# A transformer block's prelude in single words and another order, two small products on GpSimd, and the last MLP batch in halves

## The chip, the cores and the metric

The kernel runs on one core of a Trainium2 chip. Its time is the device time of one execution in microseconds (us). Five engines take part: TensorE (PE; its weight loads are listed as PEld), VectorE (DVE), ScalarE (ACT), GpSimd (POOL) and SyncE (SP), which only issues DMAs. Each engine works through its own instructions in order and waits on semaphores for the others.

## The reference

The kernel computes one block of a diffusion transformer on 16 batches of 256 tokens of width 256, all in float32: self attention with 16 heads, cross attention to a context, and an MLP of width 1024.

```python
c_proj = silu(c) @ W_mod + b_mod
shift_a, scale_a, gate_a, shift_m, scale_m, gate_m = split(c_proj, 6)
x_norm = ln(x) * (1 + scale_a) + shift_a
q, k, v = split(x_norm @ W_qkv + b_qkv, 3)            # 16 heads of 16
attn = softmax(q @ k.T * scale) @ v
x = x + gate_a * (attn @ W_proj + b_proj)
q_c = ln(x) @ W_qc + b_qc;  k_c, v_c = split(ln(context) @ W_kvc + b_kvc, 2)
x = x + (softmax(q_c @ k_c.T * scale) @ v_c) @ W_cproj + b_cproj
x_norm2 = ln(x) * (1 + scale_m) + shift_m
x = x + gate_m * (gelu(x_norm2 @ W_mlp1 + b_mlp1) @ W_mlp2 + b_mlp2)
```

## The kernel before, in words

**Units and beats.** The work is cut into 32 attention units (self attention of batch 0 to 4 first, units 0 to 4, then self and cross attention in turn). Each unit has eight beats, (n, 0) to (n, 7). In the beats of unit n the scores of unit n + 1 are multiplied (`s_tile`, row maxima by DVE into `mx`), the transposed scores of unit n (`t_part`) go to the exponential on ACT, and projections and transposes of later units fill PE. After every fourth beat the products with the values follow (tile `o`). Beats (-1, 0) to (-1, 7) hold unit 0's scores alone: at even beats both score tiles lie in the two banks of `st` and one DVE maximum of 1024 columns takes them, at odd beats they lie in `sp` with two maxima of 512.

**Precision by halves.** Each float32 operand is split into a high and a low part of a faster type, and three products are added (`mm3`). For the scores, K and Q of a unit are stacked in one tile, `big[n % 3]`: rows for high, high again and low parts, a row of ones, and a row that takes the negated row maxima. A stack is filled by DMA from the tiles `h_...` and `l_...`: six copies of 128 KB for K and six for Q. In the words of the prelude, `x` and `y` are the two copies of the high part, `l` that of the low part, and 0 or 1 the half of the heads; a `p` at the end means that GpSimd issues the copy instead of the sync queue. Unit 2 and later units send theirs in their beats.

**The prelude** is written out by hand in the string `PRE`, whose words call functions one after another, and in the table `SL`, whose words run after the beat that is their key. All engines keep the order of these words. The words that matter:

- `b12`, `b4`, `b9`, ...: so many 128x128 products of a zero tile (`busy`, two instructions each);
- `load`, `ld2`, `ld3`, `ld4`: the first weight and x loads; `z0kp`, `z1qp`, ...: GpSimd clears half of a `big` tile; `one0`: the rows of ones;
- `L0a`, `L0b`, `L0c`/`L0d`: a layernorm's statistics (DVE), mean and power (DVE, then GpSimd: `rs_s`), and its application (`c` on GpSimd, `d` on DVE: `xn_s`);
- `T0t`, `T0h`, `T0l`/`T0p`: transpose (PE), scaled high part (ACT), low part (DVE, or ACT and GpSimd);
- `scale`, `shift`, `bq`, `bk`, `bv`, `mods`: sixteen-column products for modulation and biases (`cols`: PE, then one DVE add); `sc1` and `sc2` add one on DVE;
- `hik`, `lok`, ...: split of a weight (ACT, then GpSimd; `lov` on DVE);
- `K0a`, `K0m`, `K0h`, `K0l`: first and second half of the K projection (PE, six matmuls each), high part (ACT), low part (DVE); `K1b` is `m` and `h` in one; likewise Q; `V0a`, `V0b`: values;
- `M0`: transpose of the row maxima, ACT, and their send by the sync queue; `wm`, `gm`: the MLP gate's loads, and its product.

`rest` takes the next step of a generator, `setup_rest`: loads of W_mod's gate columns, W_proj, W_cproj and biases; the attention gate `ga`; the bias product `pb` with a multiply by the gate and a store to `gd`; `cb`; loads of the cross attention's weights; and five weight splits on GpSimd. The multiplies of gate and bias (16x256, tile `gb` in `setup_rest`, tile `gB` in `f_gm`) run on DVE.

**The MLP** works in chunks (b, c), four to a batch. `mlp_second` adds chunk after chunk into `m.po`, two PSUM banks, one for each half of the tokens: those of `sp` (two tiles) for even batches and of `st` (one tile) for odd ones. After the last chunk DVE multiplies each half by the gate (`mt`), adds the residual (`y`), and one DMA of 256 KB stores the batch.

Where the trace shows L51, that is the line of the helper which issues every ordered instruction; tiles tell the instructions apart.

Of the kernel before, what the change touches and what calls it, by code (L numbers as in the profile page):

```python
# [21 lines left out]
def pixart_block(  # L22
# [8 lines left out]
    B, N, H = x.shape  # L31
# [3 lines left out]
    NT = N // P  # L35
    KC = H // P
# [58 lines left out]
    BMOD, BQKV, BQC, BKVC, BM1 = 0, 12, 18, 20, 24  # L95
# [5 lines left out]
    def tok(ap, b):  # L101
        return ap[b].rearrange("(t p) h -> p t h", p=P)
# [33 lines left out]
    st = psum.tile([P, 2, 512], F32, tag="st", name="st", bufs=1)  # L136
    sp = [psum.tile([P, 512], F32, tag=f"s{r}", name=f"s{r}", bufs=1) for r in range(2)]
# [73 lines left out]
    def setup_rest():  # L211
        gb = work.tile([B, 2, 2, H], F32, tag="pt", name="gb", bufs=5)
        gA, bb = gb[:, 0], gb[:, 1]
        bc = const.tile([1, H], F32, name="bc")
        wg, wp = stage(W_mod, 2 * H, "wga", "g", 3), stage(W_proj, 0, "wp_f", "g", 3)
        SP.dma_start(bb[:, 0], b_mod[2 * H:3 * H].partition_broadcast(B))
        SP.dma_start(bb[:, 1], b_proj.partition_broadcast(B))
        SP.dma_start(bc, b_cproj.partition_broadcast(1))
        wcp = stage(W_cproj, 0, "wcp_f", "x1", 7)
        yield  # L220
        pst = ps_gen("ps_ga")
        for k in range(KC):
            PE.matmul(pst[:B, :H], sT[:, k], wg[:, k], start=(k == 0), stop=(k == KC - 1))
        DVE.tensor_tensor(gA[:, 0], pst[:B, :H], bb[:, 0], ALU.add)
        yield
        pst = ps_gen("ps_pb")
        for k in range(KC):
            PE.matmul(pst[:B, :H], bqkv[:, 4 + k], wp[:, k], start=(k == 0), stop=(k == KC - 1))
# [3 lines left out]
        yield  # L232
        pst = ps_gen("ps_cb")
        for k in range(KC):
            PE.matmul(pst[:1, :H], bT[:, BKVC + 2 + k:BKVC + 3 + k], wcp[:, k],
                      start=(k == 0), stop=(k == KC - 1))
        DVE.tensor_tensor(bc, pst[:1, :H], bc, ALU.add)
        SP.dma_start(cd, bc)
        yield
        wkc, wqc = stage(W_kvc, 0, "wkc_f", "g", 3), stage(W_qc, 0, "wqc_f", "c", 2)  # L240
        wvc = stage(W_kvc, H, "wvc_f", "x1", 7)
        yield
        split(Wp[0], Wp[1], wp)
        yield
        split(Wkc[0], Wkc[1], wkc)
        yield
        split(Wqc[0], Wqc[1], wqc)
        yield
        split(Wvc[0], Wvc[1], wvc)
        yield  # L250
        split(Wcp[0], Wcp[1], wcp)

    wm = []

# [427 lines left out]
    def side(home, r):  # L685
        return home[r] if isinstance(home, (list, tuple)) else home[:, r]
# [164 lines left out]
    NCH = NF // 2  # L851
# [98 lines left out]
    for u in units:  # L950
        build_pre(u)
        build_post(u)
    at = defaultdict(list)
    rest = setup_rest()

    u0, u1 = units[:2]
    def one_rows(i):
# [3 lines left out]
    u2 = units[2]  # L961
    word = {}
# [45 lines left out]
    word["rest"] = lambda: next(rest, None)  # L1008
    word["vone"] = lambda: [POOL.memset(v[:, :, :, HD:], 1.0) for v in vts]
    for n, f in (("load", f_load), ("silu", f_silu), ("turn", f_turn), ("brow", f_brow),  # L1010
                 ("scale", f_scale), ("sc1", f_sc1), ("shift", f_shift),
                 ("wm", f_wm), ("mods", f_mods), ("sc2", f_sc2), ("gm", f_gm)):
        word[n] = f
    for i in range(3):
# [8 lines left out]
    for i in range(3):  # L1023
        b = i if i < 2 else 0
# [159 lines left out]
    last, o, q = units[-1], units[-1].post, units[-2].post  # L1184
# [86 lines left out]
```

## Time and profile before

| | us |
|---|---|
| median of three runs | 743.31 |
| the three runs | 748.72, 743.31, 743.25 |
| the profiled execution, its time | 744.65 |
| its span in the profile | 742.9 |

The span runs from the first to the last instruction in the profile; the execution's time holds what lies around it too. The mean granted clock of TensorE over the span is 0.999. The page has 25,296 instructions, and PE's 10,144 matmuls carry the time. The rows that are shown below have one of these forms: in the chain of waits "start, length, what"; in the timeline "start, length, engine, line, operation, tiles, count", and in square brackets the idle time before it and what ended it; in the groups "count | busy us, mean ns | idle before"; in the table of stretches the window, its length, and for each engine its busy time with the number of instructions, then the granted clock, the DMA engines' share and GB/s.

### The profile page before, as it was taken

The numbers are of one execution on the slowest core, as the hardware profiler recorded it, in microseconds if no ns is written. First come the engines' busy times: TensorE is split into PE (matmuls) and PEld (weight loads), VectorE is DVE, ScalarE is ACT, GpSimd is POOL, SyncE is SP. The second block draws the span as 40 slices with busy tenths as digits, with TensorE's granted clock in tenths as the row PEclk, the third lists the DMA queues.
The fourth block names the chain that finished last, engine by engine and source line by source line (L and its number), as shares of the span: only waits on it lengthen the run. The fifth ranks groups of instructions, "written<-read, shape, count | busy, mean of one in ns | idle before, by whom it ended". The sixth has DMA issues, their size and how long they took to land.

```text
span 742.9 us, 25296 instructions
## 1 busy us (share of the span) xinstructions
PE 733.8 (99%) x10144; PEld 648.6 (87%) x10144; DVE 575.4 (77%) x1188; ACT 564.0 (76%) x979; POOL 538.3 (72%) x569
## 2 busy tenths in 40 slices
PE   9999999999999999999999999999999999999997
PEld 8778888888888888888888888888889999999997
DVE  4888888888889898888989888888726566666662
ACT  3268898888888888888888888898886666666663
POOL 6757678869687686968769798798647766666652
PEclk9999999999999999999999999999999999999999
DMA  6754454543545454354545545455113122131310
GB/s 203 203 147 136 127 144 131 143 117 103 154 114 153 131 144 140 94 165 113 149 133 143 158 125 159 122 155 151 59 60 101 58 69 76 55 86 44 86 57 30
DMA packets 89049, 87.98 MB, mean 118 GB/s; under 512 B 8610, under 2 KB 84676, under 8 KB 88932
## 3 DMA queue, kind: packets, MB, share of 16 engines
q1 hardware_dynamic: 88468, 85.58, 40.8%
q8 instruction: 80, 1.31, 0.8%
q0 software_dynamic: 192, 0.52, 0.3%
q10 hardware_dynamic: 272, 0.26, 0.1%
q14 instruction: 37, 0.30, 0.1%
HBM read 26.97 MB, written 8.46 MB: 48 GB/s over the span
## 4 chain that ended last, share of the span: by engine, by line
PE 93%; DVE 2%; POOL 2%; DMA 1%; issue 1%; ACT 1%; SPq 0%; POOLq 0%; DVEq 0%; ACTq 0%
PE s L51 18%; PE st L51 16%; PE o L51 16%; PE ph L51 11%; PE ps_qc L51 4%; PE ps_q L51 4%; PE ps_kc L51 3%; PE ps_v_c L51 3%; PE ps_P_s L51 3%; PE ps_k L51 3%; PE ps_v_s L51 2%; PE ps_P_c L51 2%; PE psT_q L51 1%; PE psA_s L51 1%; PE psT_m L51 1%; PE ps_h L51 1%
## 5 line engine op out<-in xcount | busy, mean ns | idle before, releaser
L51 DVE TENSOR_REDUCE mx<-s 128x2 f32<-128x512 f32 x504 | 324.7, 684 | 64.5 <-PE s L51 58.1
L51 ACT ACTIVATE pt<-st 128x1024 f32<-128x1024 f32 x252 | 258.9, 1027 | 17.3 <-PE st L51 11.6
L51 PE MATMUL s<-big 63*128 63x256 f32 (+1 forms) x1024 | 184.8, 298 | 0.7 <-DVE mx L51 0.6
L51 PEld LDWEIGHTS s<-big 63*128 63x128 f32 (+1 forms) x1024 | 133.4, 186 | 20.0 <-DVE l_kc L51 6.6
L51 PE MATMUL st<-big 64*128 64x256 f32 (+1 forms) x1024 | 134.3, 298 | 0.3 <-ACT pt L51 0.2
L51 POOL TENSOR_TENSOR hl<-hf,hh 128x512 fp32r<-128x512 f32 x64 | 84.6, 1325 | 64.8 <-ACT hh L51 64.7
L51 PE MATMUL o<-pt,v 128*32 128x256 f32 x2048 | 123.8, 382 | 0.0
L51 PEld LDWEIGHTS st<-big 64*128 64x128 f32 (+1 forms) x1024 | 96.2, 185 | 15.8 <-issue 12.9
L51 PEld LDWEIGHTS o<-pt,v 128*32 128x32 f32 x2048 | 60.0, 109 | 41.5
L51 ACT ACTIVATE hf<-ph,bT 128x256 f32<-128x256 f32 x114 | 47.8, 473 | 27.6 <-PE ph L51 27.6
L51 ACT ACTIVATE hh<-ph,bT 128x256 fp32r<-128x256 f32 x114 | 47.8, 471 | 22.5 <-PE st L51 11.8
L51 ACT COPY oT<-o 128x512 f32<-128x512 f32 x63 | 36.9, 586 | 33.3 <-PE o L51 33.3
L51 DVE TENSOR_SCALAR xn_m<-x,mv_m,rs_m 128x256 f32<-128x256 f32 x28 | 24.0, 901 | 32.4 <-POOL rs_m L51 32.4
L51 PE MATMUL s<-big,hh 128*128 128x256 f32 x256 | 46.7, 281 | 0.0
L51 PE MATMUL st<-big,hh 128*128 128x256 f32 x256 | 46.6, 281 | 0.0
L51 PE MATMUL ph<-wkch,wself 128*128 128x256 f32 x224 | 44.9, 284 | 0.0
L51 PE MATMUL ph<-wqch,wself 128*128 128x256 f32 x224 | 44.7, 284 | 0.0
L51 PE MATMUL ps_k<-xTh_s,wself 64*128 64x256 f32 (+1 forms) x232 | 43.9, 295 | 0.0
L51 PE MATMUL ps_q<-xTh_s,wself 64*128 64x256 f32 (+1 forms) x240 | 39.7, 283 | 0.4 <-DVE l_q L51 0.4
L51 POOL TENSOR_SCALAR xn_c<-c,mv_c,rs_c 128x256 f32<-128x256 f32 x32 | 39.0, 1227 | 1.7
L51 PE MATMUL ps_P_s<-wself,xTh_as 64*128 64x256 f32 x256 | 39.1, 282 | 0.0
L51 PEld LDWEIGHTS st<-big,hh 128*128 128x128 f32 x256 | 39.0, 188 | 0.0
(244 smaller groups left out, 2516.9 us busy)
## 6 DMA issues: line engine op xcount, KB each, us to landing
big<-h_kc SPq DMA_DIRECT2D x64, 128.0 KB
big<-h_qc SPq DMA_DIRECT2D x64, 128.0 KB
big<-h_k SPq DMA_DIRECT2D x62, 128.0 KB
big<-h_q SPq DMA_DIRECT2D x62, 128.0 KB
big<-l_k SPq DMA_DIRECT2D x32, 128.0 KB
big<-l_q SPq DMA_DIRECT2D x32, 128.0 KB
g<-gd SPq DMA_DIRECT2D x16, 256.0 KB
c<-in_ctx_dram SPq DMA_DIRECT2D x16, 256.0 KB
```

The costliest lines, as they stand in the source:

```text
L51: i = f(*a, **k)
```

## The change

The generator `setup_rest` becomes single functions, each with a word of its own: `lg`, `lp`, `lc`, `lx` (loads), `ga`, `pb`, `gs`, `cb`, and `sp0` to `sp4` (splits). `PRE` and `SL` get another order. In it:

- unit 0's stack is cleared after `load`; the loads of `rest` and x2 are spread over the prelude;
- T0t stands before `scale`; the zero products are b12, b4, b5, b3, b9 in place of b12, b4, b4, b9;
- L1d stands behind `bk`; L2a and L2b stand in the prelude before unit 1's low parts;
- GpSimd clears unit 1's stack (`z1qp`, `z1kp`) around its copy of K0; its two copies of Q0 (`Q0y0p`, `Q0y1p`) come behind both and behind L2's power;
- of unit 1's twelve copies two are issued before the beats, the others in beats (-1, 0) to (-1, 4), the last of them (`Q1l1`) behind M0's send; all of them go by the sync queue;
- `bv` and V0a stand before Q1; K2a moves from beat (-1, 5) to (-1, 6), `sc2` to (0, 2), `z2qp` to (-1, 7); the splits run in beats (0, 0), (0, 2), (0, 3), (0, 6) and (1, 4).

The two multiplies of gate and bias go from DVE to GpSimd. In `mlp_second` the banks of even and odd batches are swapped, and for the last batch each half of the tokens is multiplied, added and stored by itself, between the matmuls of the two halves.

```diff
-'PRE': 'z0qp z0kp load rest ld2 one0 silu b12 brow L0a turn L0b b4 L0d scale T0t sc1 hik lok L1a T0h L1b T0l b4 shift hiq K0a L1d bk loq K0m K0h K0x0 K0x1 K0y0p K0y1p T1t K0l T1h K0l0 K0l1 bq T1l Q0a Q0m Q0h Q0x0 Q0y0p Q0x1 Q0y1p Q0l Q0l0 Q0l1 z1kp z1qp K1a K1b hiv lov Q1a Q1b K1x0 K1x1 K1y0 K1y1 K1l K1l0 K1l1 Q1x0 Q1x1 Q1y0 Q1y1 Q1l Q1l0 Q1l1 L2a L2b L2c V0a V0b bv b9 ld3'
-'SL': {(-1, 0): 'V1a', (-1, 1): 'T2t T2h T2p vone z2kp z2qp', (-1, 2): 'V1b', (-1, 3): 'rest wm', (-1, 4): 'M0 rest one1 ld4', (-1, 5): 'K2a L3a', (-1, 6): 'K2m L3b L3p L3c', (-1, 7): 'mods sc2 one2 rest', (0, 0): 'gm rest', (0, 1): 'rest', (0, 4): 'rest', (0, 6): 'rest', (1, 0): 'rest', (1, 5): 'rest'}
+'PRE': 'load z0kp silu b12 turn brow L0a z0qp L0b b4 L0d T0t hik scale lok sc1 lg L1a b5 T0h L1b T0l ld2 one0 shift b3 K0a bk hiq lc L1d lp L2a K0m loq K0h T1t K0y0p T1h K0l K0x0 bq hiv K0l0 T1l z1qp K0x1 K0l1 Q0a Q0m K1a K0y1p lov Q0h Q0l Q0x1 K1b Q0l0 bv z1kp V0a Q0l1 Q0x0 Q1a Q1b L2b Q1y0 K1x0 V0b K1l b9 Q0y0p Q0y1p Q1l'
+'SL': {(-1, 0): 'L2c ld3 K1l0 K1y1', (-1, 1): 'Q1l0 T2t Q1y1 V1a T2h Q1x0 K1l1 K1x1 T2p', (-1, 2): 'wm V1b Q1x1 z2kp vone', (-1, 3): 'ga K1y0', (-1, 4): 'pb M0 Q1l1 ld4 gs L3a', (-1, 5): 'L3b L3p one1', (-1, 6): 'one2 K2a L3c K2m', (-1, 7): 'z2qp mods cb', (0, 0): 'gm lx sp0', (0, 2): 'sp1 sc2', (0, 3): 'sp3', (0, 6): 'sp2', (1, 4): 'sp4'}
...
-        DVE.tensor_tensor(gA[:, 1], pst[:B, :H], bb[:, 1], ALU.add)
-        DVE.tensor_tensor(gA[:, 1], gA[:, 1], gA[:, 0], ALU.mult)
-        SP.dma_start(gd[:, 0:2], gA)
+        DVE.tensor_tensor(gA[0][:, 1], pst[:B, :H], gA[1][:, 1], ALU.add)
+
+    def f_gs():
+        POOL.tensor_tensor(gA[0][:, 1], gA[0][:, 1], gA[0][:, 0], ALU.mult)
+        SP.dma_start(gd[:, 0:2], gA[0])
...
-        DVE.tensor_tensor(gB[:, 1], gB[:, 1], gB[:, 0], ALU.mult)
+        POOL.tensor_tensor(gB[:, 1], gB[:, 1], gB[:, 0], ALU.mult)
         SP.dma_start(gd[:, 2:4], gB)
...
-            m.po = [side((sp, st)[b % 2], t)[:, :H] for t in range(NT)]
+            m.po = [side((st, sp)[b % 2], t)[:, :H] for t in range(NT)]
+        done = c == NCH - 1
+        if done:
+            t1 = work.tile([P, NT, H], F32, tag="t1", name=f"mt_{b}")
+            y = work.tile([P, NT, H], F32, tag="x1", name=f"y_{b}", bufs=7)
         for t in range(NT):
             mm3_tok(m.po[t], hT, t, [W2[0][:, 2 * c:2 * c + 2], W2[1][:, 2 * c:2 * c + 2]],
-                    kn=2, start=(c == 0), stop=(c == NCH - 1))
-        if c == NCH - 1:
-            t1 = work.tile([P, NT, H], F32, tag="t1", name=f"mt_{b}")
+                    kn=2, start=(c == 0), stop=done)
+            if done and b == B - 1:
+                DVE.tensor_tensor(t1[:, t], m.po[t], m.g[:, 0], ALU.mult)
+                DVE.tensor_tensor(y[:, t], m.xg[:, t], t1[:, t], ALU.add)
+                SP.dma_start(tok(out, b)[:, t], y[:, t])
+        if done and b < B - 1:
             for t in range(NT):
                 DVE.tensor_tensor(t1[:, t], m.po[t], m.g[:, 0], ALU.mult)
-            y = work.tile([P, NT, H], F32, tag="x1", name=f"y_{b}", bufs=7)
             DVE.tensor_tensor(y, m.xg, t1, ALU.add)
             SP.dma_start(tok(out, b), y)
```

More of the change, by code (lines that the diff above doesn't have):

```diff
@@ new lines, in pixart_block @@
+    E_ = {'CUT': 8, 'LN': {'s': 'pool', 'c': 'pool', 'q': 'pool'}, 'ON': (1, 1, 1), 'L0': -16, 'L1': 1, 'S0': -7, 'A0': 0, 'T0': 1, 'S1': 5, 'A1': 7, 'L2': 9, 'T1': 9, 'S2': 32, 'AP': 23, 'DV': (0, 1), 'HP': (1, 0), 'BZ': {}, 'AV': {1: [(1, 2), (1, 3)], 9: [(0, 0), (0, 1)]}, 'AHEAD': (0, 0, 0, 0, 0, 2), 'TW': {(21, 6): 'cb', (23, 5): 'u0', (23, 7): 'u1', (25, 2): 'u2', (27, 3): 'u3', (27, 7): 'h2a', (28, 0): 'l2 h0p u5', (28, 2): 'h1p', (28, 4): 'h3p', (28, 7): 'u4 u6', (29, 0): 'l3d', (29, 1): 'l0', (29, 2): 'l1', (29, 7): 'h5p', (30, 1): 'u7 h6d h7p', (30, 3): 'h4p', (31, 1): 'l4 l6d', (31, 2): 'l5d x2', (31, 4): 'l7', (31, 7): 'b2'}, 'BE': 'G0 av P g0 A1 G1 G2 N1 F7 g1 S0 PF s2 G3 aT aL p2 a2 G4 x3 b3 S1 S2 T2 C r0 G5 S3 G6 S4 s3 CF x4 F8 g2 G7 S5 F9 p3 S6 G8 a3 r1 G9 F10 G10 T3 g3 b4 S7 s4 F11 S8 S9 F12 G11 p4 a4 F13 r2 S10 G12 x5', 'XP': 1, 'IL': 1, 'MF': 0, 'SH': 4, 'RAMP': 1, 'HA': 1, 'MP': 16, 'W': (7, 1, 0, 0), 'PRE': 'load z0kp silu b12 turn brow L0a z0qp L0b b4 L0d T0t hik scale lok sc1 lg L1a b5 T0h L1b T0l ld2 one0 shift b3 K0a bk hiq lc L1d lp L2a K0m loq K0h T1t K0y0p T1h K0l K0x0 bq hiv K0l0 T1l z1qp K0x1 K0l1 Q0a Q0m K1a K0y1p lov Q0h Q0l Q0x1 K1b Q0l0 bv z1kp V0a Q0l1 Q0x0 Q1a Q1b L2b Q1y0 K1x0 V0b K1l b9 Q0y0p Q0y1p Q1l', 'SL': {(-1, 0): 'L2c ld3 K1l0 K1y1', (-1, 1): 'Q1l0 T2t Q1y1 V1a T2h Q1x0 K1l1 K1x1 T2p', (-1, 2): 'wm V1b Q1x1 z2kp vone', (-1, 3): 'ga K1y0', (-1, 4): 'pb M0 Q1l1 ld4 gs L3a', (-1, 5): 'L3b L3p one1', (-1, 6): 'one2 K2a L3c K2m', (-1, 7): 'z2qp mods cb', (0, 0): 'gm lx sp0', (0, 2): 'sp1 sc2', (0, 3): 'sp3', (0, 6): 'sp2', (1, 4): 'sp4'}}
@@ L209, in f_lo, with f_loads_g @@
         (POOL if i < 2 else DVE).tensor_tensor(w[1], (wq, wk, wv)[i], w[0], ALU.subtract)
-    def setup_rest():
+    gA = []
+    def f_loads_g():
         gb = work.tile([B, 2, 2, H], F32, tag="pt", name="gb", bufs=5)
[L213 to L220, printed above, removed]
+        gA.extend([gb[:, 0], gb[:, 1], stage(W_mod, 2 * H, "wga", "g", 3)])
+        SP.dma_start(gA[1][:, 0], b_mod[2 * H:3 * H].partition_broadcast(B))
@@ L221, in setup_rest, with f_loads_p, f_loads_c, f_ga @@
+    def f_loads_p():
+        gA.append(stage(W_proj, 0, "wp_f", "g", 3))
+        SP.dma_start(gA[1][:, 1], b_proj.partition_broadcast(B))
+    cB = []
+    def f_loads_c():
+        cB.extend([const.tile([1, H], F32, name="bc"), stage(W_cproj, 0, "wcp_f", "x1", 7)])
+        SP.dma_start(cB[0], b_cproj.partition_broadcast(1))
+    def f_ga():
         pst = ps_gen("ps_ga")
         for k in range(KC):
-            PE.matmul(pst[:B, :H], sT[:, k], wg[:, k], start=(k == 0), stop=(k == KC - 1))
@@ L224, in setup_rest, with f_pb @@
-        DVE.tensor_tensor(gA[:, 0], pst[:B, :H], bb[:, 0], ALU.add)
-        yield
+            PE.matmul(pst[:B, :H], sT[:, k], gA[2][:, k], start=(k == 0), stop=(k == KC - 1))
+        DVE.tensor_tensor(gA[0][:, 0], pst[:B, :H], gA[1][:, 0], ALU.add)
+    def f_pb():
         pst = ps_gen("ps_pb")
         for k in range(KC):
-            PE.matmul(pst[:B, :H], bqkv[:, 4 + k], wp[:, k], start=(k == 0), stop=(k == KC - 1))
-        DVE.tensor_tensor(gA[:, 1], pst[:B, :H], bb[:, 1], ALU.add)
-        DVE.tensor_tensor(gA[:, 1], gA[:, 1], gA[:, 0], ALU.mult)
@@ L236, in setup_rest @@
                       start=(k == 0), stop=(k == KC - 1))
[L237 to L250, printed above, removed]
@@ L251, in setup_rest, with f_loads_x, f_split @@
-        split(Wcp[0], Wcp[1], wcp)
+        DVE.tensor_tensor(cB[0], pst[:1, :H], cB[0], ALU.add)
+        SP.dma_start(cd, cB[0])
+    def f_loads_x():
+        cB.extend([stage(W_kvc, 0, "wkc_f", "g", 3), stage(W_qc, 0, "wqc_f", "c", 2),
+                   stage(W_kvc, H, "wvc_f", "x1", 7)])
+    def f_split(i):
+        w = (Wp, Wkc, Wqc, Wvc, Wcp)[i]
+        split(w[0], w[1], (gA, cB, cB, cB, cB)[i][(3, 2, 3, 4, 1)[i]])
     wm = []
@@ L953, in pixart_block @@
     at = defaultdict(list)
-    rest = setup_rest()
     u0, u1 = units[:2]
@@ L1007, in pixart_block @@
     word["M0"] = lambda: m_part(u0, 0)
-    word["rest"] = lambda: next(rest, None)
+    for i in range(5):
+        word[f"sp{i}"] = lambda i=i: f_split(i)
     word["vone"] = lambda: [POOL.memset(v[:, :, :, HD:], 1.0) for v in vts]
```

8 lines of the change are left out of this document (5 added, 3 removed).

## The prediction, made before the changed kernel was run

> **What bounds the kernel now.** I read the page first, then the chain of waits, then a table of stretches. PE (TensorE) is busy for nearly the whole span, at full granted clock, and carries nearly the whole chain; a few steps of other kinds lie early in it:
>
> ```profile
> PE 733.8 (99%) x10144; PEld 648.6 (87%) x10144; DVE 575.4 (77%) x1188; ACT 564.0 (76%) x979; POOL 538.3 (72%) x569
> ...
> PE 93%; DVE 2%; POOL 2%; DMA 1%; issue 1%; ACT 1%; SPq 0%; POOLq 0%; DVEq 0%; ACTq 0%
> ...
> 24.44 2.45 POOL xn_s L51 x2
> ...
> 40.85 1.05 DVE gB L51
> ...
> 47.32 1.86 PE o L51 x32
> ...
> 24.28:37.88 13.60, 12.98 (x90) 8.78 (x89) 11.93 (x21) 3.15 (x8) 10.22 (x12) 1.00 0.61 183
> ...
> 37.88:47.24 9.36, 8.46 (x91) 6.69 (x90) 7.96 (x14) 5.57 (x9) 5.02 (x6) 1.00 0.54 156
> ...
> 53.24:59.24 6.00, 6.00 (x76) 4.94 (x78) 5.07 (x10) 4.77 (x7) 5.80 (x7) 1.00 0.32 90
> ```
>
> The columns of the stretches are: length, then busy time of PE, its weight loads, DVE, ACT and POOL. From 53 us on PE has no idle time. So the change can act in two places only: how early the regular loop is reached, after which a shift is carried to the end unchanged, and what follows the last matmul. I split the start into the prelude up to the first score matmul (24.29), unit 0's score stage (to 37.88, beats -1,0 to -1,7) and unit 0's first five beats (to 47.24).
>
> **Prelude: PE's order and four more zero products.** The prices, from the chain, the timeline and the tile view of `big`:
>
> ```profile
> 8.12 0.80 PE st L51 x8
> ...
> 9.40 0.89 PE s L51 x8
> ...
> 11.09 0.80 PE ps_k L51 x6
> ...
> 6.48 0.74 DVE L51 TENSOR_SCALAR xn_s<-x,mv_s,rs_s 128x256 f32<-128x256 f32 x2 [2.02 <-POOL rs_s L51]
> ...
> 10.94 0.36 PE L51 MATMUL ps_k<-xTh_s,wself 128*128 128x256 f32 x1
> ...
> 11.37 1.27 POOL L51 TENSOR_TENSOR wself<-wf,wself 128x512 fp32r<-128x512 f32 x1
> ...
> 11.44 1.68 DVE L51 TENSOR_SCALAR xn_s<-x,mv_s,rs_s 128x256 f32<-128x256 f32 x2
> ...
> 13.34 0.60 PE L51 MATMUL psT_s<-ident,xn_s 128*128 128x128 f32 x4
> ```
>
> The zero products go from 12+4+4+9 to 12+4+5+3+9, four more. Each is two instructions, so at 0.89 us for eight they cost 0.9. T0t and scale change places, which moves no PE time. So K0a starts at 10.94 + 0.9 = 11.8. With K0a, bk and K0m at 0.8 each, bk ends at 13.4 and K0m at 14.2. L1d now stands on DVE behind bk's add (about 0.2 with its wait), so it runs from 13.7. Its two operations took 1.68 us beside GpSimd's split of a weight and 0.74 without; GpSimd's second split now comes before it (11.8 to 13.1), so I take 0.74, to 14.45. Behind the waiting L1d stand L2a, K0l and T1l, and T1t waits for it: T1t ends at 14.9, where it ended at 13.94, a shift of 1.0. Then bq 0.8, Q0a and Q0m 1.5, K1a and K1b 1.6 and bv 0.8 put the end of bv at 19.6.
>
> ```profile
> 17.05 1.04 POOL L51 DMA_DIRECT2D big<-h_q  x2 [1.40 <-ACT h_q L51]
> ...
> 18.08 3.58 POOL L51 MEMSET big<- 128x2048 f32 x2
> ...
> 22.10 2.25 PE L51 MATMUL s<-wz 128*128 128x128 f32 x18
> ...
> 23.62 0.72 POOL L51 TENSOR_TENSOR rs_s<-rs_s,mhalf 128x2 f32<-128x2 f32 x1
> ...
> 24.29 0.50 PE L51 MATMUL st<-big 63*128 63x256 f32 x4
> ...
> 20.36 2.51 SPq L51 DMA_DIRECT2D big<-h_k  x4
> ...
> DMA to landing us min/median/max: 3.3/5.0/5.1
> ```
>
> **The GpSimd queue.** Two of Q0's six copies (Q0y0, Q0y1) are issued by GpSimd. Before, they went out at 17.05, ahead of the memsets of unit 1. Now they stand behind both memsets and behind L2's power, which waits for L2b on DVE, behind bv's add. From bv's end at 19.6: two DVE steps to 20.2, power 1.0 to 21.2, two issues of 0.52, so the second goes out at 21.8. GpSimd's four such copies took 3.3 to 5.1 us to land, median 5.0. I take 3.3, the one that was issued into idle DMA engines, since in the new order the sync queue has nothing between Q0x0 (about 20.8) and Q1's first copy (22.6, when Q1's high part is ready). So the last copy lands at 25.1, or at 26.9 by the longest row. PE has V0a, Q1a, Q1m, V0b and the nine zero products (2.25 at most) until then: 19.6 + 3.2 + 2.1 = 24.9. The second head group of the first score tile thus waits for DMA: first scores are complete about **0.8 us later** than now (bounds +0.6 and +2.6).
>
> [...]
>
> **Score stage of unit 0.** Here DVE's row maxima follow one another, with the small products between them:
>
> ```profile
> 24.83 1.23 DVE L51 TENSOR_REDUCE mx<-st 128x4 f32<-128x1024 f32 x1 [1.54 <-PE st L51]
> ...
> L51 DVE TENSOR_REDUCE mx<-s 128x2 f32<-128x512 f32 x8 | 5.1, 675 | 0.2
> ...
> L51 DVE TENSOR_REDUCE mx<-st 128x4 f32<-128x1024 f32 x4 | 4.8, 1212 | 2.0 <-PE st L51 2.0
> ...
> L51 DVE TENSOR_TENSOR gb<-gb 16x256 f32<-16x256 f32 x1 | 0.4, 414 | 0.0
> ...
> 26.94 0.55 PE L51 MATMUL psT_s<-ident,xn_s 128*128 128x128 f32 x3 [0.56 <-POOL xn_s L51]
> ```
>
> The gate-and-bias product (0.4) leaves DVE, and the stall of 0.56 goes: L2c now follows Q0's copies on GpSimd (22.4 to 24.8) and is done before T2t. From 24.83 to 37.2 that is 12.4 us now and 11.5 to 12.0 then. But PE has nearly as much there (12.98 of 13.60), with the weight products of mods and cb last, so I count **-0.6** (0 to -1.0).
>
> Sync queue: unit 1's copies move from 20.36 on to 22.6 on. Eleven of them (0.63 each), four loads and two small ones (0.5 each) and the row-maximum copy stand before Q1l1, which goes out at about 33.3, behind a send that waits for M0. It lands at 36.6 to 38.4; unit 1's first scores need it at about 38.2. No cost by the shorter, 0.2 by the longer. The staged loads that move later (bc, wcp, wp, x2) have their first reader after 26 us.
>
> **Unit 0's beats.** The other product, gB, is on the chain itself:
>
> ```profile
> 40.41 0.40 DVE L51 TENSOR_TENSOR gB<-ps_gm,gB 16x256 f32<-16x256 f32 x1
> ...
> 40.85 1.05 DVE L51 TENSOR_TENSOR gB<-gB 16x256 f32<-16x256 f32 x1
> ...
> 41.83 1.27 DVE L51 TENSOR_REDUCE mx<-s 128x2 f32<-128x512 f32 x2
> ...
> 42.56 0.38 PE L51 MATMUL s<-big 63*128 63x256 f32 x1 [0.35 <-DVE mx L51]
> ...
> 43.15 0.50 PE L51 MATMUL s<-big 63*128 63x256 f32 x3 [0.22 <-DVE mx L51]
> ...
> 43.98 1.02 ACT L51 ACTIVATE pt<-st 128x1024 f32<-128x1024 f32 x1 [2.12 <-PE st L51]
> ...
> 45.80 0.61 POOL L51 CAST xTh_s<-y_s 128x512 fp32r<-128x512 f32 x1 [4.18 <-ACT y_s L51]
> ```
>
> Without its 1.05 us the two maxima end at 42.1 in place of 43.1. PE, which waited for them twice, is free of its query lanes at 42.05 and sets off there. The second of its two waits ended at 43.15, so the exponential that began at 43.98 comes 0.9 sooner. What is late next is ACT, which then runs without a gap, so I count **-0.9** (0 to -1.05). On GpSimd the product stands behind the memset of Q2 (1.8) and before Wp's split; nothing reads it before the MLP, and its store on the sync queue has only weight loads behind it that are read after 47 us. GpSimd's idle 4.18 us covers product, memset and split; if that cover were gone, T3's low part would be late by what overhangs. sc2 and the earlier splits have readers much later: nothing.
>
> **The end.** The last batch's two halves get a bank each, and each half its own multiply, add and store:
>
> ```profile
> 732.01 5.68 PE st L51 x48
> ...
> 737.72 0.76 DVE L51 TENSOR_TENSOR mt<-st,gm 128x256 f32<-128x256 f32 x2 [4.24 <-PE st L51]
> ...
> 738.51 0.69 DVE L51 TENSOR_TENSOR y<-xmg,mt 128x512 f32<-128x512 f32 x1
> ...
> 739.23 0.38 SPq L51 DMA_DIRECT2D out_dram<-y  x1
> ...
> 8.00:10.00 2.00, 2.00 (x21) 2.00 (x20) 0.94 (x4) 0.47 (x2) 1.05 (x1) 1.00 1.06 360
> ```
>
> Six matmuls take 5.68/8 = 0.71, so the first half is ready at 737.0. Its multiply (0.38) and add (half of 0.69, 0.35 to 0.40) end at 737.8, its issue at 738.2. The second half starts at 737.8 and ends at 738.55: the last issue comes **0.65** sooner. It carries 128 KB in place of 256; at the 360 GB/s of the busiest stretch that is up to 0.36 less, at least nothing. I take 0.15, **-0.8** in all (-0.65 to -1.0). For other batches only the banks swap, with the same distance between their uses.
>
> **The sum.** +0.8 - 0.6 - 0.9 - 0.8 = **-1.5 us**. The profiled execution took 744.65 us, its span 742.9; it would take 743.15. It lies 1.34 above the median of 743.31, so the forecast is **741.8 us**.
>
> [...]
>
> **The rivals.**
> - *The copies of Q0 land late* (slower than before). Place: first score tile; price: landing minus 25.1; it decides from 26.6 on, where it has eaten the 1.5. For it: three of four such copies took 4.9 to 5.1. Against: those ran among copies issued every 0.6 us. At 26.9 the time is 743.6; with PE's stage work not pulled in either, 744.2. I put it at 743.9, chance 0.22.
> - *Unit 0 is bound elsewhere*: another chain (ACT's exponentials, T3) takes the product's place at once and 0.9 is lost: 742.7. For: ACT runs without a gap from 43.98. Against: its idle 2.12 us just before. Chance 0.18.
> - *The start gains more*: copies landing early and the full 1.0 in the score stage: 741.2; chance 0.12.
> - *The halves do nothing*, since DVE takes up the first half only when both are done: 742.6; against it speak two separate bank tiles. Chance 0.05.
>
> **How the numbers follow.** The forecast has 0.40; 0.03 is left for something unforeseen on either side. A change of 1% (7.4 us) is about what a measurement of this kernel can tell from none. All cases lie within 2.5 us of the median, and PE's idle time in the two stretches of the start is only 0.6 and 0.9 us, so faster by over 1% gets 0.02, slower 0.03, within it 0.95. The forecast's own range is 740.8 to 742.8; with the bounds and the late copies it is 739.9 to 744.3.
>
> **What would show it.** First score matmul complete near 25.3, with a wait on the big<-h_q copies; the row maxima without a gap until 37.2; no DVE product gB, and the third beat's scores near 42; the first o group near 46.6 in place of 47.32; two stores at the end, the second issued 0.65 us sooner relative to the last matmul. It is wrong if the first o group is later than 47.3, or if the regular loop's spacing of 8 us changes.

## The result, and the profile after

The changed kernel took 741.75 us in the median of 20 runs (741.01 to 744.52), the kernel before 743.87 us in 20 runs on the same chip (742.55 to 748.72). The ratio is 0.9974, with a 95% interval of 0.9966 to 0.9982: 1.9 us less, 0.26%, which is no change by the bound of 1% and yet clear of zero. The profiled execution of the changed kernel took 741.67 us, close to its median. The one before (744.65) lay 0.8 above the 20-run median of its kernel, so the two profiles differ by 3.0 us where the medians differ by 2.1. What follows uses the profiles for the places and the medians for the prices.

The page after, first the busy time of each engine and then the chain's share by engine:

```profile
PE 732.6 (99%) x10152; PEld 648.9 (88%) x10152; DVE 572.3 (77%) x1187; ACT 564.0 (76%) x979; POOL 540.0 (73%) x571
...
PE 95%; POOL 1%; DVE 1%; ACT 1%; issue 1%; DMA 0%; SPq 0%; POOLq 0%; ACTq 0%
```

The stretches after, cut at the same events as before (first score matmul, first scores of unit 1, first o group, second o group). Columns: length, then PE, weight loads, DVE, ACT, POOL, the granted clock, DMA:

```profile
24.27:36.52 12.25, 12.25 (x91) 8.73 (x90) 11.06 (x19) 3.26 (x8) 8.28 (x11) 1.00 0.77 219
36.52:44.80 8.28, 7.96 (x92) 6.55 (x91) 6.99 (x14) 5.58 (x9) 6.18 (x7) 1.00 0.41 112
44.80:53.26 8.46, 8.18 (x113) 6.62 (x112) 7.10 (x17) 6.18 (x10) 6.54 (x9) 1.00 0.75 221
```

The score stage is 12.25 long in place of 13.60, and PE has no idle time left in it. Unit 0's beats are 8.28 in place of 9.36. The third stretch is new in the account: from first to second o group it is 8.46, where it had been 8.05 (47.25 to 55.30). The chain of waits tells where:

```profile
22.34 2.01 PE s L51 x18
24.34 0.43 PE st L51 x4
...
41.54 1.03 ACT pt L51
...
44.87 1.86 PE o L51 x32
...
49.99 0.53 SPq L51
50.61 1.88 DMA big<-m
52.49 0.14 issue
52.63 0.35 PE st L51
...
734.43 0.43 DVE mt L51
...
734.89 0.43 DVE y L51
```

The first scores follow the zero products without a wait for a copy. The first o group stands at 44.87 in place of 47.32. Then a DMA is on the chain which was not there before: the send of unit 1's row maxima (`big<-m`), issued at 50.61.

GpSimd's rows hold its two copies of Q0 and the two products that it took over; the last line is the time from issue to landing of these two copies (tile `big`, window 20 to 27):

```profile
20.96 1.11 POOL L51 DMA_DIRECT2D big<-h_q  x2
...
31.66 0.72 POOL L51 TENSOR_TENSOR gb<-gb 16x256 f32<-16x256 f32 x1
...
39.53 0.73 POOL L51 TENSOR_TENSOR gB<-gB 16x256 f32<-16x256 f32 x1 [0.77 <-DVE gB L51]
...
DMA to landing us min/median/max: 2.4/2.4/2.5
```

And the end, last issue:

```profile
736.13 0.34 SPq L51 DMA_DIRECT2D out_dram<-y  x1
```

The last matmul ended at 735.09, so the last issue came 1.04 us behind it, where it had been 1.55 (739.23 behind 737.68). From the last matmul to the end of the span it is 4.25 us in place of 5.19.

### The profile page after: what moved, and what is told of

It reads as the page before. It is cut to its first block, busy times and chain, and to the rows that moved or that the text cites. A ratio compares the mean times of both kernels' runs of the same rounds, so it can differ in the third digit from the quotient of the medians.

```text
span 739.3 us, 25308 instructions
## 1 busy us (share of the span) xinstructions
PE 732.6 (99%) x10152; PEld 648.9 (88%) x10152; DVE 572.3 (77%) x1187; ACT 564.0 (76%) x979; POOL 540.0 (73%) x571
## 3 DMA queue, kind: packets, MB, share of 16 engines
HBM read 26.97 MB, written 8.46 MB: 48 GB/s over the span
## 4 chain that ended last, share of the span: by engine, by line
PE 95%; POOL 1%; DVE 1%; ACT 1%; issue 1%; DMA 0%; SPq 0%; POOLq 0%; ACTq 0%
PE s L51 18%; PE o L51 16%; PE st L51 16%; PE ph L51 11%; PE ps_q L51 5%; PE ps_qc L51 4%; PE ps_v_c L51 3%; PE ps_kc L51 3%; PE ps_P_s L51 3%; PE ps_k L51 3%; PE ps_P_c L51 2%; PE ps_v_s L51 2%; PE psT_q L51 1%; PE psT_m L51 1%; PE ps_h L51 1%; PE psA_s L51 1%
## 5 line engine op out<-in xcount | busy, mean ns | idle before, releaser
L51 PEld LDWEIGHTS s<-big,hh 128*128 128x128 f32 x256 | 39.0, 188 | 0.0
```

Source lines behind the costliest of these rows:

```text
L51: i = f(*a, **k)
```

## The experiments

The kernels ran in groups, each with its own runs of the kernel before on the same chip, and a median is set against those. "First o" and "spacing" are the first o group and its distance to the second in the profile; "tail" is the time from the last matmul to the end of the span.

| kernel | median us (runs) | before us (runs) | ratio, 95% interval | first o | spacing | tail |
|---|---|---|---|---|---|---|
| before | | | | 47.25 | 8.05 | 5.19 |
| changed | 741.75 (20) | 743.87 (20) | 0.9974 [0.9966, 0.9982] | 44.80 | 8.46 | 4.25 |
| order_only | 743.58 (11) | 743.83 (35) | 0.9997 [0.9989, 1.0006] | 46.62 | 8.02 | 5.29 |
| before_gB_pool | 742.78 (11) | 743.83 (35) | 0.9986 [0.9978, 0.9995] | 46.10 | 8.03 | 5.18 |
| after_gB_dve | 742.06 (11) | 743.83 (35) | 0.9980 [0.9971, 0.9988] | 46.92 | 8.03 | 4.28 |
| after_end_whole | 742.68 (12) | 743.83 (35) | 0.9988 [0.9980, 0.9997] | 45.52 | 8.74 | 5.30 |
| all_but_order | 742.19 (11) | 743.67 (29) | 0.9978 [0.9969, 0.9987] | 46.25 | 8.27 | 3.90 |
| after_again | 741.90 (7) | 743.67 (29) | 0.9972 [0.9961, 0.9983] | 45.32 | 8.97 | 4.27 |
| no_b5_b3 | 743.92 (11) | 743.67 (29) | 0.9999 [0.9990, 1.0009] | 46.94 | 8.54 | 4.27 |
| copies_late | 743.91 (11) | 743.67 (29) | 0.9996 [0.9985, 1.0006] | 48.78 | 8.01 | 4.26 |
| loads_late | 741.04 (5) | 744.27 (15) | 0.9960 [0.9946, 0.9974] | 45.38 | 8.04 | 3.94 |
| warm_mods | 742.81 (11) | 744.27 (15) | 0.9981 [0.9972, 0.9990] | 46.58 | 8.04 | 4.26 |
| split_mods | 744.44 (12) | 743.99 (16) | 1.0002 [0.9985, 1.0020] | 49.17 | 8.02 | 3.94 |
| loads_late_2 | 740.48 (6) | 743.99 (16) | 0.9946 [0.9930, 0.9963] | 45.26 | 8.02 | 4.04 |

### One part at a time

**order_only**: the new order alone; both products back on DVE, the last batch as before (its lines, those shown at after_end_whole, are left out here).

```diff
-        POOL.tensor_tensor(gA[0][:, 1], gA[0][:, 1], gA[0][:, 0], ALU.mult)
+        DVE.tensor_tensor(gA[0][:, 1], gA[0][:, 1], gA[0][:, 0], ALU.mult)
...
-        POOL.tensor_tensor(gB[:, 1], gB[:, 1], gB[:, 0], ALU.mult)
+        DVE.tensor_tensor(gB[:, 1], gB[:, 1], gB[:, 0], ALU.mult)
```

> The changed order alone: both products back on DVE, the end of the MLP as before. Theory A (the parts add up, each at its own place): first score matmul near 24.3 us, first scores of unit 1 near 36.9 (one product of 0.4 more in the score stage), gB's multiply again between gate sum and maxima, so the first o group near 46.2, 1.1 before that of the kernel before; time about 1.0 us under before. Theory B (the order only makes room that DVE's products would fill again): first o group at 47.0 or later, time within 0.3 us of before.

It gave 0.25 us, within its interval of nothing; of the two theories the median fits the second. Yet unit 1's first scores stood at 36.84, 1.04 sooner than before, as the first had it; at the first o group 0.63 of that was left. Something that neither had named showed in the stretches, here cut at 3.42 us; the column to read is the granted clock, third from the end:

```profile
33.30:36.72 3.42, 3.21 (x24) 2.40 (x23) 2.87 (x7) 0.65 (x2) 2.80 (x4) 1.00 0.68 192
36.72:40.14 3.42, 3.42 (x17) 1.70 (x18) 2.60 (x6) 1.29 (x2) 3.33 (x4) 0.50 0.11 33
40.14:43.56 3.42, 3.21 (x39) 2.96 (x40) 2.90 (x6) 1.24 (x2) 0.84 (x1) 1.00 0.62 164
```

For 3.42 us TensorE's granted clock was 0.50. None of the profiles of the kernel before or of the changed one shows such an interval between the first scores and the last matmul, so the prediction could not see it. It is followed up below; it does not account for the small gain, since the two of eleven runs at a mean clock of 0.999 or more took 743.37 and 743.95.

**before_gB_pool**: the kernel before, with gB's product alone on GpSimd.

```diff
-        DVE.tensor_tensor(gB[:, 1], gB[:, 1], gB[:, 0], ALU.mult)
+        POOL.tensor_tensor(gB[:, 1], gB[:, 1], gB[:, 0], ALU.mult)
```

> The kernel before with gB's multiply alone on GpSimd. Theory A: first scores of unit 1 stay at 37.9, the two waits of PE for mx after 42 us go, first o group near 46.4 in place of 47.3; time 0.9 us under before. Rival (the gain needs the new order): first o group at 47.0 or later, time within 0.3 us of before.

It gave 1.05 us, and its first o group stood 1.15 sooner than before's: the product's time on the chain, nearly in full.

**after_gB_dve**: the changed kernel, with that one product back on DVE.

```diff
-        POOL.tensor_tensor(gB[:, 1], gB[:, 1], gB[:, 0], ALU.mult)
+        DVE.tensor_tensor(gB[:, 1], gB[:, 1], gB[:, 0], ALU.mult)
```

> The changed kernel with gB's multiply back on DVE, all else kept. Theory A: the first scores of unit 1 stay at 36.5, the maxima of beat (0, 1) start 1.05 later and the first o group comes near 45.8 in place of 44.9; time 0.9 us over the changed kernel. Rival (unit 0 is bound by ACT's exponentials or by T3): first o group stays within 0.2 us of 44.9 and so does the time.

The median is only 0.3 above the changed kernel's, where 0.9 was expected. In its profile the product took 1.50 us, beside the subtraction of GpSimd's split (38.93 to 40.22), and PE waited for the maxima behind it; then the clock fell (first row: length 3.41, PE busy 2.43):

```profile
38.99 1.50 DVE L51 TENSOR_TENSOR gB<-gB 16x256 f32<-16x256 f32 x1
...
41.15 0.38 PE L51 MATMUL s<-big 63*128 63x256 f32 x1 [0.77 <-DVE mx L51]
...
38.33:41.74 3.41, 2.43 (x20) 2.02 (x20) 3.33 (x5) 1.02 (x1) 1.80 (x2) 1.00 0.26 66
41.74:45.15 3.41, 3.40 (x33) 3.41 (x35) 1.70 (x4) 1.87 (x3) 0.00 (x0) 0.50 0.73 199
```

So the same product is worth 1.05 in the old order and about 0.3 in the new one. One reason shows in the spacings: in the new order the spacing is 8.03 with the product on DVE, and 8.46 and 8.97 in the two profiles of the changed kernel. Half a microsecond or more of what unit 0 gains is lost again one unit later.

**after_end_whole**: the changed kernel, with `mlp_second` as before.

```diff
-            m.po = [side((st, sp)[b % 2], t)[:, :H] for t in range(NT)]
+            m.po = [side((sp, st)[b % 2], t)[:, :H] for t in range(NT)]
...
-            if done and b == B - 1:
-                DVE.tensor_tensor(t1[:, t], m.po[t], m.g[:, 0], ALU.mult)
-                DVE.tensor_tensor(y[:, t], m.xg[:, t], t1[:, t], ALU.add)
-                SP.dma_start(tok(out, b)[:, t], y[:, t])
```

> The changed kernel with the end of the MLP as before: no halves, banks as before. Theory A: nothing changes up to the last matmul; from the end of PE's last matmul to the end of the span 5.2 us in place of 4.2; time 0.9 to 1.0 us over the changed kernel. Rival (the second store's issue and landing eat the gain): within 0.3 us of the changed kernel.

The halves are worth 742.68 - 741.75 = 0.93. The tail says the same in every profile: 5.18 to 5.30 with one store, 3.90 to 4.28 with two.

**all_but_order**: the kernel before, with both products on GpSimd and the new `mlp_second` (its lines, those of the change, are left out here).

```diff
-        DVE.tensor_tensor(gA[:, 1], gA[:, 1], gA[:, 0], ALU.mult)
+        POOL.tensor_tensor(gA[:, 1], gA[:, 1], gA[:, 0], ALU.mult)
...
-        DVE.tensor_tensor(gB[:, 1], gB[:, 1], gB[:, 0], ALU.mult)
+        POOL.tensor_tensor(gB[:, 1], gB[:, 1], gB[:, 0], ALU.mult)
```

> The kernel before, with its old order of the start, and with the change's three other parts: both gate and bias products on GpSimd, the last batch in halves. Theory (the three parts add to what they gave one at a time, and the new order gives only what it gave alone, 743.58 against 743.83, -0.25): the product of gB -1.05 (742.78 against 743.83), the halves -0.93 (742.68 against 741.75), the product of gb 0 to -0.6, so 741.3 to 741.9, level with the changed kernel. Rival (the order's gain is real but shows only once the products are off VectorE: unit 1's first scores stood at 36.52 after and at 37.88 before, 1.36 us): about 742.8, 1 us over the changed kernel. Deciding: 742.3 lies between. Tail after the last matmul 4.2 to 4.3 instead of 5.2.

742.19 lies on the theory's side of 742.3, 0.3 over its upper end. With the changed kernel at 741.75 to 741.90, the new order is worth 0.3 to 0.4 beside the other parts and 0.25 alone, in both cases less than the intervals can tell apart.

**after_again** is the changed kernel itself, beside all_but_order.

> The changed kernel once more, for a second profile and for comparisons on this chip. It should come to 741.75 within 0.3. If the interval of 3.4 us at a granted clock of 0.50 comes by chance of phase, some of its runs show a mean clock of 0.996 to 0.998 (8 of 20 did so far) and others 0.999 to 1.0, and the first differ from the second by less than 0.6 us; if it belongs to the other orders alone, no run shows it.

741.90, as expected. Five of its seven runs have a mean clock of 0.997 or 0.998; their median is 741.90, and the other two are 740.90 and 741.93. By the mean clock the interval at 0.50 belongs to this kernel too; that is an inference, since neither of its two profiles caught one.

### The zero products and the late copies

**no_b5_b3**: the changed kernel without the words b5 and b3.

```diff
-... sc1 lg L1a b5 T0h L1b T0l ld2 one0 shift b3 K0a bk ...
+... sc1 lg L1a T0h L1b T0l ld2 one0 shift K0a bk ...
```

> The changed kernel without the groups of five and of three zero products ahead of the first projection. They compute nothing that is used. Theory (the first projection waits for the low half of the first rows, which VectorE ended at 11.45, so the zero products were cover): the first projection starts within 0.2 of 11.6 and the time stays within 0.3 of the changed kernel's 741.75. First rival (the prediction's term, four zero products at 0.22 of path): about 0.9 less, 740.9. Second rival (the granted clock, which was 0.50 for 3.4 us once in three of the four runs so far, follows how little TensorE had to do): with eight products fewer between 6 and 11.5 us, a stretch of 3.4 us at 0.50 appears near 10 to 15 us, and the time is 0.5 to 1.7 longer, 742.3 to 743.4.

The second rival. With less to do, the kernel took 2.0 us more. The first projection did start sooner, at 10.18, though its second matmul waited for the low half until 10.94. Then:

```profile
10.94 0.39 PE L51 MATMUL ps_k<-xTl_s,wself 128*128 128x256 f32 x1 [0.40 <-DVE xTl_s L51]
...
9.30:12.72 3.42, 3.02 (x24) 2.83 (x25) 2.03 (x9) 1.35 (x3) 2.16 (x3) 1.00 0.71 228
12.72:16.14 3.42, 3.42 (x19) 3.42 (x18) 2.32 (x7) 2.18 (x5) 1.40 (x2) 0.50 0.09 22
16.14:19.56 3.42, 3.42 (x17) 3.42 (x18) 1.57 (x4) 0.50 (x3) 3.42 (x3) 0.50 0.78 209
19.56:22.98 3.42, 3.42 (x31) 3.42 (x31) 1.98 (x7) 1.19 (x3) 0.94 (x3) 1.00 0.42 111
```

Two intervals follow one another, 6.83 us at half clock, and the first score comes at 26.42 in place of 24.27. Nine of eleven runs have a mean clock of 0.995 or less, median 744.22. The two runs without took 741.34 and 741.87, no less than the changed kernel's 741.64 at that clock. So far as two runs can tell, the eight products are cover at full clock, as the theory said; what they pay is the clock.

**copies_late**: GpSimd's memset of the ones in `v` moved ahead of its two copies of Q0.

```diff
-PRE: ... b9 Q0y0p Q0y1p Q1l      SL (-1, 2): 'wm V1b Q1x1 z2kp vone'
+PRE: ... b9 vone Q0y0p Q0y1p Q1l SL (-1, 2): 'wm V1b Q1x1 z2kp'
```

> The changed kernel with GpSimd's memset of the values' ones moved ahead of its two copies of Q0, so that the copies are issued about 1.45 us later, at 22.4 instead of 20.96. They then land near 24.9 and 25.5 instead of 23.36 and 24.00, and the nine zero products end at 24.34. Theory (the first scores are the later of the two, and what is late there is late at the end): the first score at 25.4 to 25.6 with a wait for the DMA on its row, +1.1, and 742.7 to 743.0. Rival (unit 0's beats have slack that takes it back): first score as late, but the first o group less than 0.6 later than 44.8 and the time within 0.5 of the changed kernel's.

It missed on both sides: +2.0 against the changed kernel beside it. The copies were issued from 22.00 on and landed in 2.8 and 3.3, and the first scores waited as expected:

```profile
25.04 0.35 PE L51 MATMUL st<-big 63*128 63x256 f32 x1 [1.11 <-issue]
25.95 0.58 PE L51 MATMUL st<-big 63*128 63x256 f32 x2 [0.56 <-DMA big<-h_q]
```

The second row's matmuls last 0.58 where a pair lasts 0.4: the clock fell at 25.96, after PE's idle 1.67, and again at 39.6, each time for 3.4 us. The four runs at a mean clock of 0.999 have a median of 742.22, 0.6 over the changed kernel's ten at full clock (741.64); the seven others 744.13. So the delay itself costs about half of the 1.1 expected, between theory and rival, and the larger price is that of the clock.

### The send that was late, and the narrow products

The sync queue of the changed kernel around the second half of unit 1's maxima, whose row on ACT comes first:

```profile
48.20 0.25 ACT L51 ACTIVATE m<-psm 16x128 fp32r<-16x128 f32 x1
...
42.82 0.42 SPq L51 DMA_DIRECT2D wkc_f<-in_L_xcond_W_kvc_dram  x1
43.68 0.40 SPq L51 DMA_DIRECT2D wqc_f<-in_L_xcond_W_qc_dram  x1
44.13 1.26 SPq L51 DMA_DIRECT2D wvc_f<-in_L_xcond_W_kvc_dram  x1
45.44 1.21 SPq L51 DMA_DIRECT2D big<-l_k  x2
46.76 2.47 SPq L51 DMA_DIRECT2D big<-h_q  x4
49.33 1.19 SPq L51 DMA_DIRECT2D big<-l_q  x2
50.61 0.57 SPq L51 DMA_DIRECT2D big<-m  x1
```

The maxima were ready at 48.45. The queue has hardly a gap, and their send waits 2.2 us in it. Three loads stand at its head; TensorE first reads their split halves at 96 us. **loads_late** moves these loads and their splits by one unit:

```diff
-(0, 0): 'gm lx sp0', (0, 2): 'sp1 sc2', (0, 3): 'sp3', (0, 6): 'sp2', (1, 4): 'sp4'
+(0, 0): 'gm sp0', (0, 2): 'sc2', (1, 1): 'lx', (1, 4): 'sp4 sp1', (1, 6): 'sp3', (2, 0): 'sp2'
```

> The changed kernel with the three loads of weights for the cross attention, and their splits, moved from unit 0's beats to unit 1's. In two profiles of the changed kernel the row maxima of unit 1's second half were ready at 48.45 and 48.97, but their send was issued at 50.61 and 51.66, behind the copies of unit 2's queries on the sync queue, and landed at 52.49 and 53.52; TensorE waited for it 0.26 and 0.32, and the first two o groups stood 8.46 and 8.97 apart, against 8.05 before. The three loads and their waits take the queue from 42.82 to 45.39. Theory (the queue is the bound there): the send is issued about 1.5 us sooner, TensorE's wait for it is gone, the o groups stand 8.0 to 8.2 apart, and the time is 0.3 to 0.8 less than the changed kernel's 741.75 to 741.9, so 741.0 to 741.5. Rival (VectorE's maxima or the products end last there anyway): the o groups stay 8.4 or more apart and the time stays within 0.2.

The theory held. The send goes out 0.8 behind its data (49.03 to 49.81), TensorE's wait is gone, the spacing is 8.04, and the median of 741.04 is under both kernels', with all five runs at a mean clock of 0.997. On another occasion it gave 740.48, with one such run of six:

> The kernel with the late loads once more, beside the split. It should come to 741.04 within 0.3, and to 0.3 to 0.9 less than the changed kernel; if the five runs at a mean clock of 0.997 were its rule, nearly all of these show that clock too.

That missed on all three counts: 0.6 below 741.04, 1.3 below the changed kernel, and the low clock is not its rule. Its ratio of 0.9946 [0.9930, 0.9963] does not overlap the changed kernel's, that of the first occasion does. In the profile of loads_late the clock falls here:

```profile
33.19 1.96 PE L51 MATMUL ps_mods<-sT,wmod 128*128 128x16 f32 x16
35.08 1.65 PE L51 MATMUL ps_cb<-wcp_f,bT 128*1 128x256 f32 x4
...
32.07:35.48 3.41, 3.41 (x28) 2.88 (x27) 3.32 (x8) 0.84 (x2) 2.34 (x4) 0.98 0.70 209
35.48:38.60 3.12, 3.12 (x15) 1.46 (x14) 1.52 (x3) 0.47 (x2) 2.79 (x2) 0.50 0.59 142
```

The clock fell at 35.34, 0.14 before the cut. TensorE counts as busy for all of the 3.41 us before. But 16 of the matmuls have 16 columns only (128x16 in the row), and the four behind them, begun at 35.08, have weights of one column (128*1). **warm_mods** tests whether that is the cause, by four zero products (word d4) on each side:

```diff
-(-1, 7): 'z2qp mods cb'
+(-1, 7): 'z2qp d4 mods d4 cb'
```

> The changed kernel with four zero products on each side of the sixteen products of 16 columns that make the later modulation rows, 33.7 to 35.5 in the profile. They compute nothing that is used, and take 8 times 0.107 = 0.86 us of TensorE. Theory (the 3.4 us at a granted clock of 0.50 in the changed kernel's slower runs follow this stretch of narrow products, as they did at 36.7 with the order alone and at 35.8 with the end as before): the share of runs with a mean clock of 0.998 or less, 15 of 27 in the changed kernel so far, falls to 2 or fewer of about 11, and the time is 0.3 to 0.9 longer, 742.1 to 742.7. Rival (the interval arises later, in unit 0's beats, where TensorE waits for maxima and exponentials): the share stays near a half, and the time is 0.9 longer or more.

None of 11 runs has a mean clock under 0.999; the changed kernel has 15 of 27, loads_late beside it five of five. The share came as the theory said, the time lies 0.1 over its range: 742.81, 0.9 to 1.1 over the changed kernel. The products cost more than was counted, since each is two instructions: unit 0's score stage took 14.13 in place of 12.25.

That narrow work is the whole cause is not shown. In the profile of the changed kernel a stretch of the same length holds all twenty of these matmuls, 33.67 to 36.52, and the clock stayed full in it and behind it:

```profile
33.55:36.96 3.41, 3.41 (x30) 2.55 (x29) 2.66 (x5) 0.57 (x2) 3.22 (x5) 1.00 0.71 204
```

**split_mods** tried to have it for nothing, on top of the late loads: the sixteen narrow products in two groups of eight.

```diff
-(-1, 5): 'L3b L3p one1', ... (-1, 7): 'z2qp mods cb'
+(-1, 5): 'mods0 L3b L3p one1', ... (-1, 7): 'z2qp mods1 cb'
```

> The kernel with the late loads, and the sixteen narrow products of the modulation rows in two groups of eight, the first moved two places ahead of the second, between first scores; one more addition on VectorE (0.22). Theory (the granted clock of 0.50, in all five runs with the late loads, follows the unbroken stretch of products with 16 columns and with one, 33.19 to 36.66 there): with the stretch cut by eight products of 0.112, 0.9 us, the mean clock is 0.999 or 1.0 in at least half of the runs, and the time is 0.2 to 0.6 less than with the late loads alone, 740.4 to 740.9. Rival (what is left of the stretch suffices): the share stays as it is and the time is level or 0.2 longer.

A plain miss, 3.4 us above the late loads at 741.04 and 4.0 above those beside it at 740.48, and for a reason that was in the trace all along: the moved group needs its weights two beats sooner.

```profile
32.75 1.86 PE L51 MATMUL ps_mods<-sT,wmod 128*128 128x16 f32 x8 [2.08 <-DMA wmod<-in_L_xcond_W_mod_dram]
```

PE waited 2.08 for them, and from within that wait, at 32.24, the clock was halved for 6.83 us. It says nothing about the theory, since it replaced narrow work by idle time.

## Why the prediction was right, and where its steps were wrong

The forecast was 741.8 and the median 741.75, but that it came so close is luck, since two errors cancel: the sum was -1.5 where the medians differ by 2.1, and the median of three runs that it was set against, 743.31, lay 0.56 under that of twenty. The mechanisms named were at work, but for the late copies; the start, the score stage and unit 0's beats were mis-sized, and unit 1 was left out. The sizes below are those of the two profiles and add up to more than 2.1. Their spans differ by 3.5, and 0.55 of that lies in the regular loop, where no term stands.

**Start, +0.8 predicted: about +0.2.** The first score came at 24.27, not 25.1, without a wait, level with the 24.29 before. But the two profiles do not start alike. TensorE reaches its full clock at 7.05 in the one before and at 6.25 in the changed one; ahead of that the instructions of the first zero products follow one another every 0.21 us, behind it every 0.11. The nearest pair is before_gB_pool and after_again (7.24 and 7.25; the preludes are those of the two kernels): there the first projection stands 0.96 later (11.03 to 11.99), which is the 0.9 that four more products were to cost, and the first score only 0.19 later (24.42 to 24.61). The sub-step that failed is "I take 3.3" for the landing: the two copies took 2.40 and 2.46, were issued from 20.96 on and not 21.2, and lay there 0.3 before the zero products ended at 24.34. The work behind bv was over-counted too, 5.3 predicted and 4.96 taken. GpSimd's copies took 3.3 to 5.1 to land in the profile before, 2.4 to 3.2 in the one after and 2.8 to 3.3 in copies_late; that range is wider than the prediction's bounds.

**Score stage, -0.6 predicted (0 to -1.0): -1.35.** The step that failed is "PE has nearly as much there (12.98 of 13.60)": PE's busy time was taken for a floor, and with the same matmuls it fell to 12.25. Most of it is the wait for `xn_s`. The rows of T2t's transposes, the first before, the others after (the end before is in the prediction's row at 26.94):

```profile
26.05 0.33 PE L51 MATMUL psT_s<-ident,xn_s 128*128 128x128 f32 x1
...
24.94 0.66 PE L51 MATMUL psT_s<-ident,xn_s 128*128 128x128 f32 x4
25.35 0.49 PE L51 MATMUL psv_s<-wself,xTh_s 128*128 128x256 f32 x2
```

From the first of them to the next product it was 1.36 (26.05 to 27.41) and is 0.41: 0.95 less, where a stall of 0.56 was counted. order_only, with the first product still on DVE, has a stage of 12.73 and after_gB_dve, without it there, of 12.25, so moving that product is worth about 0.5 in the new order; in the old order it is worth nothing (13.67 in all_but_order).

**Unit 0's beats, -0.9 predicted: -1.1.** before_gB_pool gave -1.05 of time, the whole of the product's time on the chain. "What is late next is ACT" fits: its exponential began at 41.54 with 1.04 of idle time before it, where there had been 2.12.

**Nothing predicted: +0.4 to +0.9 in unit 1.** The step that failed is "its store on the sync queue has only weight loads behind it that are read after 47 us". The loads' readers were looked at, but not the send of the maxima queued behind the loads and copies. With unit 0 a microsecond shorter, the same queue is late for it. loads_late shows it: with the loads moved the spacing is 8.04 again, and 8.02 in loads_late_2.

**The end, -0.8 predicted: -0.93.** The last issue came 0.51 sooner relative to the last matmul (0.65 predicted), and from that issue to the end of the span it was 3.22 in place of 3.64, 0.42 less, where 0.15 was taken.

**Nothing predicted: the clock.** In the profiles of all three of the first four experiments that have the new order an interval at half clock followed. It does not explain why that order, which has unit 1's scores a microsecond sooner, is worth only 0.3 to 0.4: among the runs at a mean clock of 0.999 or more, the changed kernel's ten have a median of 741.64 and all_but_order's eight 742.09, 0.4 again. With the late loads besides, the five such runs of loads_late_2 have 740.45. So the late send took more of the order's gain than the clock did; how the rest divides was not isolated.

Of the prediction's markers the first (first score near 25.3, with a wait) was wrong. The third beat's scores came near 42 and the two stores as it said, the first o group at 44.87, sooner than the 46.6 that it named. The loop kept its spacing: from the third o group to the last matmul it took 674.53 before and 673.98 after, and 673.56 to 674.60 over the other profiles.

## What to carry to other kernels

When a stage gets shorter, go through every queue that it shares with the next and ask which small send now stands last in it; here an 8 KB send behind three loads that TensorE needed only at 96 us cost about half of what a moved product gave, and moving the loads gave 0.7 to 1.3 us. Matmuls of zeros that look like waste can hold the clock: in no_b5_b3, without eight of them, nine of eleven runs had a mean clock of 0.995 or less, and the median was 2.0 us longer. Take them out only with the granted clock of many runs beside the time, since one profile may show none of it. Before moving work earlier, look up when its operands land.

## What the hardware showed that was not expected

**Half the clock for 3.4 us at a time.** Seven profiles show it, at a granted clock of 0.50: 3.4 us from 36.72 (order_only), 35.84 (after_end_whole), 41.74 (after_gB_dve), 35.34 (loads_late), and 25.96 and 39.62 (copies_late); and twice that, 6.83, from 12.72 (no_b5_b3) and 32.24 (split_mods). The mean clock that each run lists hints at which runs had it:

| kernel | runs at 0.999 or more, median us | runs at 0.998 or less, median us |
|---|---|---|
| before, beside order_only | 23, 743.76 | 12, 744.19 |
| before, beside no_b5_b3 | 16, 743.50 | 13, 744.10 |
| changed, 20 runs | 10, 741.64 | 10, 742.04 |
| no_b5_b3 | 2, 741.61 | 9, 744.22 |
| copies_late | 4, 742.22 | 7, 744.13 |
| warm_mods | 11, 742.81 | 0 |
| loads_late, loads_late_2 | 0 and 5, 740.45 | 5, 741.04 and 1, 741.64 |

For the kernel before the hint is weak. In the profiles of before and changed the clock also falls to 0.50 behind the last matmul, 3.24 and 5.03 us after it (at 740.92 and 740.12), and what lies inside the span is in the mean: before's 0.999 has 1.95 us of it and no interval. The profile of after_end_whole has a mean of 0.996, where its interval alone would make 0.998.

The groups lie 0.4 to 0.6 apart for the kernels before and changed, and 1.9 and 2.6 for copies_late and no_b5_b3, whose profiles show two intervals. The same kernel has it in some executions only, and the share can differ from one occasion to another (five of five and one of six for the late loads).

What sets the interval off was not found. In copies_late the clock fell at 25.96, behind 1.67 us of idle TensorE in two parts (1.11 and 0.56), and in split_mods at 32.24, within a wait of 2.08. In loads_late it fell at 35.34 behind 3.41 us in which TensorE counted as busy throughout, with 16 narrow products in them; in warm_mods, with eight zero products of 128x128 around the same sixteen, no mean clock of 11 runs was under 0.999. That the narrow products are the cause would fit, but the changed kernel kept a granted clock of 1.00 from 33.55 to 36.96 with the same products; what the clock follows stays open.

**One small product, four durations.** The multiply of 16x256 took 0.41 and 1.05 on DVE in the kernel before and 1.50 in after_gB_dve, and 0.72 on GpSimd. Beside the two longer ones GpSimd ran the two-input subtraction of a split (40.34 to 41.63 and 38.93 to 40.22), beside the 0.41 a memset. That this neighbour stretches it is read from the traces, not tested alone.
